# A four-layer graph network on one core: where the mean is multiplied by the reciprocal deviation, and a newly searched order of the work

## The chip, the cores and the metric

The kernel runs on one core of one Trainium2 chip. A core has five engines with queues of their own, each worked through in order: TensorE (PE in the profile; its weight loads are PEld), VectorE (DVE), ScalarE (ACT), GpSimd (POOL) and SyncE (SP), which here only issues transfers. The metric is the device time of one execution in microseconds. A measurement is the median of several executions.

## The reference

64 graphs with 256 nodes of 256 features each go through four layers. Each layer normalizes x, applies relu, and adds its result to x. Cut to what matters:

```python
def _layernorm(x, axis=-1, eps=1e-5):
    m = jnp.mean(x, axis=axis, keepdims=True)
    v = jnp.var(x, axis=axis, keepdims=True)
    return (x - m) / jnp.sqrt(v + eps)

h = jnp.maximum(_layernorm(x, axis=-1), 0.0)
x = x + _L0_gnn_ref(h, adj, ...)   # attention, 8 heads, mask from adj
h = jnp.maximum(_layernorm(x, axis=-1), 0.0)
x = x + _L1_gnn_ref(h, adj, ...)   # additive attention, softmax over axis 1, elu
h = jnp.maximum(_layernorm(x, axis=-1), 0.0)
x = x + _L2_gnn_ref(h, adj, ...)   # 3 steps of message passing and a GRU cell
h = jnp.maximum(_layernorm(x, axis=-1), 0.0)
x = x + _L3_gnn_ref(h, adj, ...)   # additive attention, 4 heads
```

So each graph is normalized four times, and a node's row needs r = 1/sqrt(v + eps) and, in one form of the scaling, also -m times r.

## The kernel before, in words

**Tiles.** Two graphs make a pair, and a pair's x is one tile of 128 partitions by 4 token groups by 256 features. The 32 pairs go through the layers 0, 1, 2 and 3. Tiles come from pools with a fixed number of buffers (6 for x, 21 for general work, `w4`, 8 PSUM banks).

**The planner.** The kernel isn't written in the order in which it runs. `Plan.add` collects tasks: an engine, a planned duration, the function that issues the instructions, and what it reads and writes. Some tasks have two forms on two engines. `Plan.ranked` decodes the string `ORDER`: three bytes for each task, two that give its place within the order and one that gives its form. `Plan.order` walks through that order once with planned durations, a time for a semaphore to reach another engine (`HOP`), a time for a transfer to land (`LANDING`, 1.2) and one port for GpSimd and those VectorE tasks that carry a `True`; from this it gives out buffers and puts filler transposes (L443) where TensorE would be idle. Then the instructions are issued in that order, each to its engine's queue. The string came from a search done outside the kernel. There are 13,776 tasks, 1788 of them TensorE's, and several pairs are under way at a time: the first TensorE task of pair 15 is number 721 of the 1788, its last is number 1013.

**Normalization** (`norm_relu`), four times for each pair, 128 times in all:

- For each of the two graphs g, VectorE computes statistics of two token groups (bn_stats, L660) and gathers them into mean and variance (bn_aggr, L662), in the tile `mv`. One task of planned 0.87 us.
- GpSimd adds eps to the variance (L673) and raises it to the power -0.5 (L674), into the first half of the tile `rs`. These are 128x4 operands, two instructions, one task of planned 1.4 us.
- VectorE multiplies the mean by -1 and by r (L679), into the second half of `rs`, a task of its own.
- x is scaled either by ScalarE as x times r plus (-m r) (L687) or by VectorE as (x - m) times r (L693).

In the last pair's layer 3 the normalization goes in two halves of two token groups each ("fine").

**After it.** In most pairs the normalized tile is transposed in blocks by VectorE (L836 and L802), written to DRAM (L791) and read back in four pieces (L794); L716 (ScalarE) or L717 (VectorE) then takes relu. L860 is the masked minimum and L867 the exponential of the attention layers. Layer 1 spreads a row to all partitions through DRAM (L1005, L1007, L1015), adds it (L1046), masks (L860), takes exponentials (L1073), divides (L1076, L1079, L1083) and multiplies on TensorE (L1096). Layer 2 holds most of the matrix work: the gates (L1219) and the messages (L1180) with their operands (L1164, L1165, L1170). L974 and L1416 are the products that read what was transposed through DRAM. Evictions of PSUM are L480 (ScalarE) and L481 (VectorE), biased ones L1235 and L1237.

**Work that may go to GpSimd.** Four additions of 512 or 256 columns are given in two forms by `either`, GpSimd or VectorE: L889 (bias in layer 0), L1282 (in the GRU), L1336 (layer 2 into x) and L1455 (layer 3 into x). The planned GpSimd time is 0.16 + 512/460 us, the planned VectorE time 0.065 + 512/960.

Of the kernel before, what the change touches and what calls it, by code (L numbers as in the profile page):

```python
# [13 lines left out]
FR = mybir.dt.float32r  # L14
# [5 lines left out]
P = 128  # L20
EPS = 1e-5
# [20 lines left out]
class Plan:  # L42
# [7 lines left out]
        "c-qBV2Y6h?)!jSudfVQ2C9SmTU2d{1x%Wl~gM)!kLJJ{;1PFly0s)fH`5_^JK!7ClUIPRhgE3$muyOCUELpv;wB^k|B4BTmy|SG|pOIFpx9`"  # L50
        "o|a_%|z4laJyhS~2__#U-mh&c*=D-ME=B}9;2Rbdvq05MpHzyzvTgzMpMfV0ut=v-$5IuF3B?O|h*5v=7ux$%poYiswfQT6gEeR;P#mugiKF"
        "5O^q^;>`eSmJ(;C%6r@$nyk?`BjS^GBvxpb-`q`^%cPUHp|BQ6e9;k^CAuIOWh#ws?BXFyjCqD0xbGu+{&rKB$y0xS@UuQ4b18U%b*!fkTAI"
        "uiMkU`Kw|InHpEy})e=I_s&Z6yy3__{3P=#<b9WjU;^+YE(xi|Y3rTc6F_!)(X!KQ+By%jpnCa^nM9elPiZN0cXLXtX94LVnD;CT`aWhzC=l"
        "~h$R>ZIE3@{q&QF{?-6eO_9JnjTd@bXy4nB`im9hztXv_+&(S49Bc8r7$4tNN$Rv)ve&Jg{u`NfD&N0Ju4Xb^$1M0S6Ib=;w8ojdB1i*g}IO"
        "NU{%TU8a^mGiwKsPh7_cJ;<ha=GfG+QtZIvD6Ho>x3x@VwPFO_4?V$oakh8Rl!J2ka7bpu13A<t#DX7XV`?`W(=?>k_8P<M=F;`~m1wL8IR+"
        "Hq&?zrqDJ0J@VWH3~GF^{82r+GS<z|QM=>^R3F(m@o9euhq>w~HIH04wMIiI=P#4hBb!dY2N%*V{>fX0XIB0=1h>-|mBM6jQtMRIpVea*SM0"
        "~jNK`&hK`#~j0m`0*Br`93F5OWxUK?z|Uq5nh{^A8XD7R{D6Ft&OvVot+WQgj~ALwb~I4N*KDD8Xx+RL|rf_O!x!?hC&8KsQbsjw#!a{8SHy"
        "p6?pB&*^qbsl+(~%8dM;`<)OPnfaDP27NUj1uffNyl~sHKg3r*o%}SFq1`-SMeiZ|cF?eDz^i#|G-Zv0fw%8T$D0QF6qg+Lu^3w}7o<}cAmR"
        "tZkV19tOOjhh|S3yKzGlrrj6E<_r0tel!8JYO%U5=gRh(l;ST~u-{+u&9dSQZeR>*oNBaz)%zmw{Qex4OGLFfO9SBC|Uo+v2l9ue4O|2Y;k3"
        "IvU`@Pb<O&9Y&tlB&N%XvQS~(j^K$e+ufZON3FR{tJ1}ys^!kY(k<n8V;(AV9Z(SKZ07>@FBu-o$dk_ngr_7YVaq)jI^Go-f~wtNmRzceBG~"  # L60
        "FJgt)ByNw?Im;M5I#RCi6JVFXZxNc2Z@Re%Cy!sKQw$wmNCQr>f5T?1?P<Si386<cCjKd`z{CI}c8b<*Zh42Dh`%qmZB4x2HD?7)XbM88D9^"
        "Iv682rsva&|Ea9axvTj6YAaTO$Gb7SI&Os95X=H)A=4Funf4Hoa8jm*4)qVLg7K~bnxb&FI^?8m+ps`XJJ2P{yyIXj2Ue1UNyFf56x=gK<E}"
        "g@Oa(hfQE(Db>^(^YXGavHVj~4JhrIrZnt&3bOp8&q!z~LddQ;Jq=;{i(r2O&;Boe&aBhPmCJIc!`7IW7G7cdQ#q?ZUf|mSE-}F1#4_<R5Y("
        "@RfkZf%YsZ#-_8}(gRmu@`mmHcQ0&%r#RGq0S)sNif<BUz9=ILRB43R?k88qD9*l2xKuCqI9OQfU2$uN3xcd_JjI2bJrAv38Df4dF`Au~)hq"
        "5OJ~m*^d$z1tSF0LaWGr(0a^J*DbdNnUk{~uHMx-dQHI&j*LbiBU@Rcm)w+(D2^@M(d2zR2t37(3SgF-m>9!M-dq$?LB@W&y9fN8W{7aIR0L"
        "b|cI3Nxx>gC=rDDJ2ecc~a9H`3<9AM0#{9ZL&)KhZGgRlegrFUGK)l^xs5#RJo-HTVwT?}>1gv;-s2!*h%01^Fu*O#6vgt2G^UxW&>s$Q7ve"
        "A3vzq|Jg%fL|L8td;)Dmm<v8>o2SbV1MDu7!@z!pcg}hbv++pSg#L%4zdCk4SXF6XV$S^_a*SU8B98a3;2_ks~yI@f`vhn(ZqSs{_HSn@>>+"
        "7@!GiCO5QGW8=s$)i^1t5O{aaWPy^_?oX<_`kPeiJ*e>w6QVm5O=yA6dZpiD*25&wEl+n~?td&Ih0Nya_d|k%Z-eu>aeyy;>5}Dg)z5UXuhz"
        "5bw&Fx@A-oM&$N4VeG!H`k7s*LWEcfeScddPI`L(zvOV>MK5%)a0O^*Z#2AO0UZrFCD89Ztb3kg-!5KtvjFX)K&I=d4cK=24S#I$eR2iPC>|"
        "U?|rv&F=usZ0+>3ws)`Gu*2p@EN6<LEWVW4R$ah~wI7VxKS$)zc9oM&s+ETK7Ma>r6Js;KHcHrP%cdUS^lIPA>lece@z?b}trY53OEo8h%1k"  # L70
# [269 lines left out]
def tile_adj_preln_d4(  # L340
# [143 lines left out]
    def either(more, do):  # L484

        return [(G, pool(N2) + more, lambda: do(nc.gpsimd), True), (V, dve(N2) + more, lambda: do(nc.vector), True)]
# [165 lines left out]
    def norm_relu(xt, p, tokens=False, turning=True):  # L652
# [3 lines left out]
        for g in range(2):  # L656

            def stats(g=g):
                for t in (2 * g, 2 * g + 1):
                    nc.vector.bn_stats(st()[:, t, :], tok(xt())[:, t, :])  # L660
                for t in (2 * g, 2 * g + 1):
                    nc.vector.bn_aggr(mv()[:, t, :], st()[:, t, :])  # L662
# [873 lines left out]
```

## Time and profile before

| what | value |
|---|---|
| median of the runs shown | 3443.62 us (4 runs, 3438.23 to 3449.06) |
| the profiled execution's own time | 3445.27 us |
| its span, first to last instruction | 3443.3 us |
| mean granted TensorE clock | 0.997 |
| TensorE busy | 3400.3 us, 99% |
| VectorE busy | 3113.5 us, 90% |
| ScalarE busy | 2450.8 us, 71% |
| GpSimd busy | 453.0 us, 13% |
| transfers | 785 MB, mean 228 GB/s |

Busy time is counted per engine; matrix instructions overlap in their pipeline, and their ends are modelled. A group line of the profile has the line of the code, the engine, the operation, the tiles and shapes and the count; behind the bar the busy time in us and the mean of one in ns; behind the second bar the time for which the engine stood idle just before these instructions, and what ended most of it. "DVE rs L679" after an arrow means: the wait ended when VectorE's instruction of line 679, which writes `rs`, was done. In a timeline, the idle time before an instruction stands in square brackets.

### The profile page before, as it was taken

The page shows a single profiled execution, that of the slowest core. Times are in us where ns is not written, and L with a number is a line of the kernel's source. Part 1 is how long each engine was busy: PE and PEld are TensorE (multiplying, and loading weights), DVE is VectorE, ACT ScalarE, POOL GpSimd, SP SyncE. Part 2 cuts the span into 40 slices and gives each one's busy share as a digit, 9 for nine tenths or more (in the row PEclk, how much of TensorE's full clock was granted, in tenths as well). Part 3 has the DMA queues.
Part 4 walks back from the last instruction along what each step waited for, and adds up shares of the span by engine and source line. Part 5 has one row for each costly group of instructions (what it writes and reads, how often), then busy time and mean ns, then how long its engine had stood idle before and what let it go on. Part 6 is the DMA issues. An engine that isn't in the chain of part 4 may idle for free. (4 is left out here: it accounts for less than half of the span.)

```text
span 3443.3 us, 55520 instructions
## 1 busy us (share of the span) xinstructions
PE 3400.3 (99%) x15701; PEld 1912.4 (56%) x15701; DVE 3113.5 (90%) x8903; ACT 2450.8 (71%) x6608; POOL 453.0 (13%) x505
## 2 busy tenths in 40 slices
PE   9999999999999999999999999999999999999998
PEld 5555555555555555555555555555555555555546
DVE  8889999998999989989999899999989999888778
ACT  8767777776677777677767776767776677766555
POOL 1100111111101111111110112111111110000100
PEclk9999999999999999999999999999999999999999
DMA  9756876887768778768778677887778776876546
GB/s 294 219 153 202 268 238 220 253 249 232 239 212 238 242 229 252 229 209 251 241 225 251 215 239 228 251 245 223 227 230 251 233 236 206 234 213 211 174 140 215
DMA packets 617687, 784.99 MB, mean 228 GB/s; under 512 B 101412, under 2 KB 524836, under 8 KB 617380
## 3 DMA queue, kind: packets, MB, share of 16 engines
q1 hardware_dynamic: 617380, 781.45, 74.0%
q8 instruction: 125, 2.05, 0.3%
q14 instruction: 182, 1.49, 0.2%
HBM read 442.51 MB, written 330.32 MB: 224 GB/s over the span
## 5 line engine op out<-in xcount | busy, mean ns | idle before, releaser
L1219 PE MATMUL ps<-w,whhT 128*128 128x512 f32 (+1 forms) x2328 | 1076.4, 591 | 2.2 <-DVE w L1293 1.1
L1219 PE MATMUL ps<-w,giT 128*128 128x512 f32 (+1 forms) x2328 | 1066.3, 588 | 0.5 <-DVE mx L860 0.3
L867 ACT ACTIVATE w<-w,mx 128x256 f32<-128x256 f32 x1536 | 758.8, 499 | 31.5 <-DVE mx L860 30.6
L1219 PEld LDWEIGHTS ps<-w,giT 128*128 128x128 f32 x2328 | 439.6, 190 | 526.1 <-issue 506.6
L1219 PEld LDWEIGHTS ps<-w,whhT 128*128 128x128 f32 x2328 | 432.7, 190 | 486.6 <-issue 439.3
L802 DVE STREAM_TRANSPOSE w<-w 128x1024 f32<-128x1024 f32 x380 | 465.9, 1230 | 31.0 <-ACT w L954 15.0
L480 ACT COPY w<-ps 128x512 f32<-128x512 f32 x476 | 267.9, 579 | 221.4 <-PE ps L1096 47.5
L860 DVE CUSTOM_DVE_ANT_0 w<-ps,mask 128x256 f32<-128x256 f32 x1024 | 373.4, 415 | 25.7 <-PE ps L922 24.3
L954 ACT ACTIVATE w<-w,rz 128x256 f32<-128x256 f32 x678 | 297.9, 500 | 83.5 <-DVE rz L948 81.0
L867 ACT ACTIVATION_READ_ACCUMULATOR w<-w,mx 128x1 f32 x1536 | 293.8, 191 | 0.0
L1282 POOL TENSOR_TENSOR w<-w,w 128x512 f32<-128x512 f32 x98 | 130.0, 1333 | 1059.1 <-ACT w L1276 835.4
L687 ACT ACTIVATE w<-x,rs 128x256 f32<-128x256 f32 x368 | 196.6, 592 | 98.3 <-DVE rs L679 95.0
L1180 PE MATMUL ps<-part,part 128*128 128x256 f32 x1536 | 252.8, 312 | 3.4 <-DVE part L1170 1.5
L1392 ACT ACTIVATE w<-w,f 128x256 f32<-128x256 f32 x512 | 224.2, 499 | 32.2 <-DMA w<-row 25.7
L1180 PEld LDWEIGHTS ps<-part,part 128*128 128x128 f32 x1536 | 201.7, 190 | 62.0 <-issue 41.3
L673 POOL TENSOR_SCALAR rs<-mv 128x4 f32<-128x4 f32 x129 | 37.2, 288 | 1481.9 <-DVE mv L662 1313.1
L1276 ACT ACTIVATE w<-w,bih_sb 128x512 f32<-128x512 f32 (+1 forms) x194 | 137.1, 712 | 113.8 <-DVE w L1272 113.2
L860 DVE CUSTOM_DVE_ANT_0 w<-w,mask 128x256 f32<-128x256 f32 x512 | 199.7, 425 | 16.9 <-ACT w L1392 15.6
L1250 ACT ACTIVATE w<-ps,brz 128x512 f32<-128x512 f32 (+1 forms) x194 | 129.9, 674 | 93.7 <-PE ps L1219 78.8
L660 DVE BATCH_NORM_STATS2 st<-x 128x6 f32<-128x256 f32 x512 | 188.8, 410 | 2.6 <-DMA x<-in_x_dram 0.5
L1264 ACT ACTIVATE w<-ps,brz 128x512 f32<-128x512 f32 (+1 forms) x194 | 130.0, 674 | 73.8 <-PE ps L1219 67.5
L1288 DVE SCALAR_TENSOR_TENSOR w<-w,w 128x512 f32<-128x512 f32 (+1 forms) x194 | 139.5, 722 | 14.8 <-ACT w L1264 9.1
(120 smaller groups left out, 5054.2 us busy)
## 6 DMA issues: line engine op xcount, KB each, us to landing
turn<-w SPq DMA_DIRECT2D x565, 512.0 KB
w<-turn SPq DMA_DIRECT2D x2260, 128.0 KB
w<-in_adj_dram SPq DMA_DIRECT2D x128, 512.0 KB
w<-row SPq DMA_DIRECT2D x64, 512.0 KB
x<-in_x_dram SPq DMA_DIRECT2D x64, 256.0 KB
out_dram<-x SPq DMA_DIRECT2D x64, 256.0 KB
turn<-w SPq DMA_DIRECT2D x62, 256.0 KB
w<-turn SPq DMA_DIRECT2D x248, 64.0 KB
```

The lines of the kernel that those rows point to most:

```text
L480: (A, act(n), lambda: nc.scalar.copy(dst(), src())),
L660: nc.vector.bn_stats(st()[:, t, :], tok(xt())[:, t, :])
L687: nc.scalar.activation(tok(xn())[:, t, :], tok(xt())[:, t, :], func, bias=rs()[:, 1, t : t + 1], scale=rs()[:, 0, t : t + 1])
L802: add((V, dve(T * N), lambda: nc.vector.transpose(blocks(), blocks())), writes=[e])
L860: nc.vector.tensor_tensor_reduce(row, src, mask, scale, 3.0e38, ALU.add, ALU.min, mn)
L867: nc.scalar.activation(row(e, r), row(e, r), AF.Exp, bias=mn()[:, r : r + 1], scale=-1.0, accum_out=zs()[:, z0(r) : z0(r) + 1])
L954: op(row(e, r), row(e, r), rz()[:, r : r + 1])
L1180: mm(ps()[:, o * N : (o + 1) * N], chunk_of(part(), h.mixed, c, o), tok(ams[g](), N)[:, c, :], start=i == 0 and c == 0, stop=i == 1 and c ...
L1219: mm(ps()[:, 0:n], w[:, k, c0 : c0 + P], of(wide(src, k)), start=i == 0, stop=i == 2 * len(terms) - 1)
L1276: (A, act(n, 1), lambda o=o: nc.scalar.activation(at(hn, o), at(hn, o), AF.Tanh, bias=bih_sb[:, 4 + o : 5 + o])),
L1288: (V, dve(n), lambda o=o, z=zt[o]: nc.vector.scalar_tensor_tensor(of(wide(u, o)), z()[:, 0:n], 1.0, of(wide(u, o)), ALU.add, ALU.mult), True),
L1392: nc.scalar.activation(dst, src, AF.Prelu, bias=f()[:, t, D + h : D + h + 1], alpha=ALPHA)
```

## The change

Four things are changed.

1. eps is added to the variance, and the mean's sign is turned, in the statistics task on VectorE: two instructions more for each graph, on 128x2 operands. The planned time goes from 0.87 to 1.0 us.
2. GpSimd's task is now the power (without the addition before it) and behind it the product of the turned mean and r, into the second half of `rs`. Its planned time goes from 1.4 to 1.7 us. The VectorE task of L679 is gone. VectorE's form of the scaling adds the turned mean where it subtracted the mean.
3. The planned time of `either`'s GpSimd form is 0.4 us longer.
4. The string `ORDER` is another one. It came from a search with GpSimd's instructions taken longer and a larger margin on every landing. `LANDING`, `HOP` and the other constants of `Plan` are as they were.

```diff
     def either(more, do):
 
-        return [(G, pool(N2) + more, lambda: do(nc.gpsimd), True), (V, dve(N2) + more, lambda: do(nc.vector), True)]
+        return [(G, pool(N2) + 0.4 + more, lambda: do(nc.gpsimd), True), (V, dve(N2) + more, lambda: do(nc.vector), True)]
...
                 for t in (2 * g, 2 * g + 1):
                     nc.vector.bn_aggr(mv()[:, t, :], st()[:, t, :])
-
-            add((V, 0.87, stats), reads=[(xt, g)], writes=[(st, g), (mv, g)])
+                nc.vector.tensor_scalar_add(mv()[:, 2 * g : 2 * g + 2, 1], mv()[:, 2 * g : 2 * g + 2, 1], EPS)
+                nc.vector.tensor_scalar_mul(mv()[:, 2 * g : 2 * g + 2, 0], mv()[:, 2 * g : 2 * g + 2, 0], -1.0)
+
+            add((V, 1.0, stats), reads=[(xt, g)], writes=[(st, g), (mv, g)])
...
             def rstd(ts=ts):
-                nc.gpsimd.tensor_scalar_add(rs()[:, 0, ts], mv()[:, ts, 1], EPS)
-                nc.gpsimd.tensor_tensor(rs()[:, 0, ts], rs()[:, 0, ts], mhalf[:, ts], ALU.pow)
+                nc.gpsimd.tensor_tensor(rs()[:, 0, ts], mv()[:, ts, 1], mhalf[:, ts], ALU.pow)
+                nc.gpsimd.tensor_tensor(rs()[:, 1, ts], mv()[:, ts, 0], rs()[:, 0, ts], ALU.mult)
 
             of = lambda b: (b, ts.start // 2) if fine else b
-            add((G, 1.4, rstd, True), reads=[of(mv)], writes=[of(rs)])
-            add(
-                (V, 0.07, lambda ts=ts: nc.vector.scalar_tensor_tensor(
-                    rs()[:, 1, ts], mv()[:, ts, 0], -1.0, rs()[:, 0, ts], ALU.mult, ALU.mult), True),
-                reads=[of(mv)], writes=[of(rs)],
-            )
+            add((G, 1.7, rstd, True), reads=[of(mv)], writes=[of(rs)])
...
                         tok(xn())[:, t, :], tok(xt())[:, t, :], mv()[:, t, 0:1], rs()[:, 0, t : t + 1],
-                        ALU.subtract, ALU.mult,
+                        ALU.add, ALU.mult,
```

The two strings, decoded with the rule in `Plan.ranked`, compare like this:

| in the order | before | changed |
|---|---|---|
| tasks | 13,776 | 13,647 |
| TensorE tasks / SP tasks | 1788 / 3611 | 1788 / 3611 |
| L889 on GpSimd / VectorE | 38 / 26 | 46 / 18 |
| L1282 on GpSimd / VectorE | 98 / 96 | 82 / 112 |
| L1336 (tasks of two instructions) on GpSimd / VectorE | 37 / 27 | 25 / 39 |
| L1455 on GpSimd / VectorE | 31 / 31 | 15 / 47 |
| biased evictions on VectorE (L1237) | 77 of 194 | 58 of 194 |
| TensorE tasks between a piece's issue (L794) and its first reader, mean | 7.23 | 7.77 |
| the same for the smaller pieces of layer 3 (L1439) | 4.30 | 5.11 |
| the same for adjacency (L772) | 7.07 | 7.28 |
| the same for spread rows (L1015) | 1.51 | 1.68 |

The first and last TensorE places of each pair differ by at most four between the two. One in twenty of the tasks has the same task behind it as before.

## The prediction

> **What bounds the kernel now.** I read the first two parts of the page, then a table of busy time over three stretches of the span, then TensorE's own waits, then the groups that the change touches, and last a timeline around the longest wait.
>
> ```profile
> span 3443.3 us, 55520 instructions
> PE 3400.3 (99%) x15701; PEld 1912.4 (56%) x15701; DVE 3113.5 (90%) x8903; ACT 2450.8 (71%) x6608; POOL 453.0 (13%) x505
> ```
>
> TensorE is busy for 3400.3 of 3443.3 us. VectorE comes next with 90%. What can be won or lost is therefore TensorE's idle time, 43.0 us, and the filler: transposes of the identity (L443) that the planner puts where it expects TensorE to stand idle.
>
> ```profile
> 0.00:200.00 200.00, 187.61 (x970) 118.02 (x971) 173.83 (x594) 148.92 (x422) 26.31 (x37) 0.98 0.81 244
> 200.00:3400.00 3200.00, 3181.94 (x14429) 1772.18 (x14428) 2904.70 (x8205) 2273.61 (x6103) 424.44 (x465) 1.00 0.74 227
> 3400.00:3443.30 43.30, 30.77 (x305) 22.25 (x304) 34.99 (x106) 28.30 (x88) 2.22 (x3) 0.94 0.74 223
> ```
>
> Each row has a stretch, its length, and then the busy time of PE, PEld, DVE, ACT and POOL. PE idles 12.4 us in the first 200 us, 18.1 us in the 3200 us between, and 12.5 us at the end. In the middle it is at 99.4%, at full clock (the column after POOL: 1.00). The filler is small:
>
> ```profile
> L443 PE MATMUL ps<-ident 128*128 128x128 f32 x85 | 10.5, 274 | 0.0
> ```
>
> So 3443.3 - 43.0 - 10.5 = 3389.8 us is matrix work. The change touches none of it: the same 1788 TensorE tasks stand in both order strings.
>
> Which wait ends last in the middle stretch? These are TensorE's waits there (us in total, times, longest):
>
> ```profile
> PE ps L1096 <- DVE dst L1373: 2.9, 1, 2.9
> PE ps L1180 <- DVE part L1170: 1.5, 3, 0.8
> PE ps L1361 <- ACT w L716: 1.5, 2, 1.0
> ...
> PE ps L1361 <- DVE w L717: 1.1, 1, 1.1
> ...
> PE ps L974 <- DMA w<-turn: 0.6, 1, 0.6
> ```
>
> They are few and short. Behind these five groups, 7.6 us, stands a transfer, directly or one step back: L716, L717 and L1165 (ahead of L1170) read what comes back through DRAM. The longest can be followed:
>
> ```profile
> 1456.58 1.70 ACT L1046 ACTIVATE w<-w,f 128x256 f32<-128x256 f32 x4 [4.05 <-DMA w<-row]
> 1463.47 0.51 ACT L1073 ACTIVATE w<-w,mx 128x256 f32<-128x256 f32 x1 [4.20 <-DVE mx L860]
> 1466.06 1.19 PE L1096 MATMUL ps<-w,w 128*128 128x256 f32 x2 [2.88 <-DVE dst L1373]
> ```
>
> ScalarE stood 4.05 us for a row from DRAM, layer 1's exponentials came late, and 9.5 us on TensorE stood 2.88 us. This is what "a larger margin on every landing" would act on.
>
> **The change part by part.** First the means times the reciprocal deviation.
>
> ```profile
> L674 POOL TENSOR_TENSOR rs<-rs,mhalf 128x4 f32<-128x4 f32 x127 | 135.2, 1065 | 10.6
> L673 POOL TENSOR_SCALAR rs<-mv 128x4 f32<-128x4 f32 x127 | 36.7, 289 | 1459.6 <-DVE mv L662 1290.8 <-DVE rz L948 85.3 <-ACT w L867 58.6
> L679 DVE SCALAR_TENSOR_TENSOR rs<-mv,rs 128x4 f32<-128x4 f32 x127 | 37.1, 292 | 39.8 <-POOL rs L674 39.6
> ```
>
> The columns after the count are busy us, mean ns of one, idle before it. *GpSimd:* it loses the addition (L673, 0.29 us) and gains a product of two 128x4 operands that the trace does not show. From below the bound is L673, 0.29 us; from above the power on the same shape, 1.065 us. I take 0.29: GpSimd's two-operand adds are 1.333 us for 512 columns (L1282) and 0.807 for 256 (L1336), a straight line that leaves 0.29 at 4 columns. So 0 (to +0.78 us) per normalization, on an engine with 13% busy.
>
> *VectorE* loses L679: 37.3 us busy in all, and 39.6 us in which its queue stood still behind L679 for GpSimd, 76.9 us together. It gains four small instructions in each of 128 normalizations, 512. The nearest rows are the three in the bias preparation:
>
> ```profile
> 115.19 0.13 DVE L594 TENSOR_TENSOR brz<-bih_sb,bhh_sb 128x4 f32<-128x4 f32 x1
> 115.36 0.17 DVE L595 TENSOR_SCALAR brz<-brz 128x4 f32<-128x4 f32 x1
> 115.44 0.16 DVE L596 TENSOR_SCALAR bhn<-bhh_sb 128x2 f32<-128x2 f32 x1
> ```
>
> From start to start an independent one takes 0.08 us (L595 to L596), one that reads the result before it 0.17 (L594 to L595). 512 of them cost 41 to 87 us; I take one of each per pair, about 0.12, so 61 us.
>
> *Forms.* The order strings say which engine takes each addition that may run on either. GpSimd's go from 204 to 168: VectorE gets 16 more of L1282 (0.685 us), 12 more of L1336 (two of 0.5 us each), 16 more of L1455 (0.745) and 8 fewer of L889 (0.673): 11.0 + 12.0 + 11.9 - 5.4 = +29.5 us. Of the evictions and scalings that ScalarE may take instead, VectorE gets 26 more copies (L481, 0.671) and 19 fewer biased ones (L1237, 0.728), which with the rest comes to about +8.
>
> *Contention.* L679 takes 157 ns in the median and up to 1246 where GpSimd works; 51 us less GpSimd work (16 x 1.333 + 24 x 0.807 + 16 x 1.34 - 8 x 1.34) can give VectorE between 0 and 51 us. I take 5, by L679's excess of (289 - 157) ns x 129 = 17 us against 172 us of GpSimd work on norms.
>
> VectorE's account: -76.9 + 61 + 29.5 + 8 - 5 = +17 us, between -49 and +48. All of it lies beside matrix work. VectorE's idle time without the waits on GpSimd is 3443.3 - 3113.5 - 39.6 = 290 us; if TensorE's 18.1 us of waits grow as that shrinks, 17/290 of them is **+1.1 us** (-3 to +3). If that cover were gone, all 17 would count.
>
> *The wait on rs.* ScalarE's scaled copies (L687) stood 95.0 us behind L679, because it sat late in VectorE's queue. Now they wait for GpSimd, right behind the power. ScalarE is 71% busy, so I count nothing; its next wait there is for VectorE's statistics. Behind a waiting L687 on ScalarE are copies out of PSUM. In the last layer, where nothing covers it, the old chain ran from GpSimd's start at 3408.19 to L693 at 3409.35. The new one adds two small VectorE instructions (0.25) and a product (0.29) and drops L673 (0.31 with its gap) and L679's 0.04: **+0.2 us** (-0.2 to +1.0).
>
> *The order.* Both strings were decoded. Pair by pair, first and last TensorE positions differ by at most four places of 1788, so the staging is the same, but only 5% of neighbours are kept. The margin can be seen: the first reader of a transposed piece (L794) stands 7.77 TensorE tasks behind its issue where it stood 7.23. At 3389.8/1788 = 1.9 us a task, that is 1.0 us more. Taking 1.0 us off each of the eight transfer-linked waits above leaves about 1.9 + 0.1 of 7.6: **-5.6 us**. For each transfer that SP issues (3611 SP tasks in both) nothing is added; the other 10.5 us of middle waits I leave as they are, though they are drawn anew.
>
> A rule of the Trainium skill speaks against the multiply's move: GPSIMD Engine Reference, section 3.1, counts 1 cycle per element on VectorE and about 2.6 on GpSimd, and keeps elementwise work on VectorE. By the rule the move only loses. In this trace L679's 289 ns on VectorE and the 289 ns that I take for GpSimd are alike at four columns, and L679's price was the 39.6 us of standing. Another speaks against the small VectorE instructions: SBUF — State Buffer, section "SBUF: two separate sides", says that a VectorE instruction in a two-port mode and a GpSimd instruction exclude each other for their whole length. By it 256 pairs, met by GpSimd in 13% of cases for half a power, would cost 256 x 0.13 x 0.53 = 18 us more of VectorE, an estimate; L679's 1246 ns agrees with its kind, and the sum would be +35 instead of +17.
>
> **The sum** is made against the profiled execution, 3445.27 us, which is 1.65 above the median of 3443.62. 3445.27 - 5.6 + 1.1 + 0.2 = 3441.0; less 1.65 that is **3439.3**, 0.13% below the median.
>
> **Rivals.** *Likeliest (0.42): no change that counts.* A measurement of this kernel can tell about 0.2%, 6.9 us; within it the time is 3436.7 to 3450.5.
>
> *Faster (0.35).* The waits that now go, VectorE's 39.6 us and ScalarE's 95.0, were also what made other feeders late, so that 8 of the remaining 12.5 us of middle waits go with them: 3445.27 - 5.6 - 8 - 1.65 = 3430. For it: nearly all of TensorE's middle waits end with VectorE or ScalarE. Against it: in the stretch from 300 to 400 us VectorE is at 96.7% and TensorE still at 99.7%, so lateness there is not what load makes. No more than the 18.1 us can go in the middle.
>
> *Slower (0.23): the additions moved to VectorE.* 44 additions (16 + 12 + 16) that GpSimd did at leisure now stand in VectorE's queue in order, 0.7 to 1.0 us each, ahead of something that TensorE reads. Place: L1282 and L1455, between gates and evictions. If one in three delays TensorE by its own 0.75 us, that is 11 us, without the landing gain 3443.6 + 11 = 3455; it decides from about one in five (6.6 us). Against it: GpSimd's adds took 1.333 us where VectorE's take 0.685, so the results come sooner.
>
> *The margin is only in the string* (inside the first case): the constant for a landing is 1.2 in both, and the readers of adjacency and of row spreads hardly moved (7.07 to 7.28 and 1.51 to 1.68 tasks). Then the 2.9 us wait may stay or return elsewhere: 3445.
>
> **How the numbers follow.** Forecast 3439.3. Range 3426 to 3458: the faster case with 4 us more, by VectorE's lower bound, and the slower one with 3 us more, by its upper one. Faster by over 0.2%: 0.35; within: 0.42; slower: 0.23.
>
> **What would show it.** GpSimd's product near 0.29 us; L679's 39.6 us of VectorE idling gone; small instructions at 0.08 to 0.17 us; GpSimd below 400 us busy; matrix work unchanged; TensorE's middle idle time near 13 us. Wrong would be a middle idle time above 25 us, TensorE waiting behind L1282 or L1455 on VectorE, or an end stretch longer than 43 us by more than 1.

## The result and the profile after

The changed kernel takes **3448.64 us** (median of 41 runs, 3445.03 to 3453.45). The kernel before, run beside it, takes 3445.22 (61 runs, 3438.23 to 3451.11). The ratio is 1.0011, with a 95% interval of 1.0006 to 1.0015: slower by about 3.4 us, where the forecast was 4.3 us faster. The profiled execution of the changed kernel took 3445.95 us, 2.7 below its median, so its trace shows only a part of the difference: its span is 0.9 us longer. The medians given below for *wide_same_plan*, *slow_gpsimd*, *new_eight_small* and *bare_new* hold one slow execution each (3555.81, 3601.02, 7649.29 and 7863.81 us), and without it they are lower by 0.4, 0.2, 0.1 and 0.5 us, which changes no reading. Line numbers moved up by one to four (L443 is now L442, L717 is L713, L794 is L790, L1219 is L1215).

The span and the engines' busy time, from the page of the changed kernel:

```profile
span 3444.2 us, 56079 instructions
PE 3407.5 (99%) x15720; PEld 1907.4 (55%) x15720; DVE 3164.6 (92%) x9350; ACT 2444.5 (71%) x6591; POOL 406.1 (12%) x457
```

TensorE's idle time fell from 43.0 to 36.7 us, and yet the span is longer: TensorE's *busy* time grew by 7.2. VectorE's grew by 51.1 us, GpSimd's fell by 46.9. By stretches, in the order of columns that the prediction explained:

```profile
0.00:200.00 200.00, 189.21 (x982) 119.63 (x983) 177.22 (x632) 145.19 (x410) 27.02 (x38) 1.00 0.79 244
200.00:3400.00 3200.00, 3185.92 (x14430) 1764.52 (x14429) 2949.86 (x8605) 2268.97 (x6089) 375.62 (x414) 1.00 0.75 227
3400.00:3444.20 44.20, 32.35 (x311) 23.26 (x310) 37.57 (x115) 30.32 (x94) 3.47 (x5) 0.95 0.68 213
```

The idle time in the middle is 3200 - 3185.9 = 14.1 us, where it was 18.1; 13 to 14 was forecast. The filler, from the groups of TensorE, is part of what TensorE gained in busy time:

```profile
L442 PE MATMUL ps<-ident 128*128 128x128 f32 x104 | 13.2, 274 | 0.0
```

That is 2.7 us more filler; the other 4.5 us are the same number of matrix instructions, taking longer in all. Like for like they take longer still. In the trace before, TensorE's granted clock was halved for 13.7 us in three places (at 45, 100 and 1465 us; the first row of the windows shows it as 0.98 before and 1.00 after), which is about 6 us of busy time lost (TensorE was busy for 12.3 of the 13.7), and the changed kernel has no such place before 3430 us. So matrix work apart from filler and clock grew by 10 to 11 us. The costliest of TensorE's waits in the middle stretch:

```profile
PE ps L1176 <- DVE part L1166: 1.4, 3, 0.9
PE ps L1215 <- DVE mx L856: 1.3, 2, 1.0
PE ps L1357 <- DVE w L713: 1.3, 1, 1.3
...
PE ps L970 <- DMA w<-turn: 0.2, 1, 0.2
```

The 2.9 us wait behind the row from DRAM is gone, and nothing above 1.3 us came in its place. The normalization's new groups (count | busy, mean ns | idle before):

```profile
L675 POOL TENSOR_TENSOR rs<-mv,rs 128x4 f32<-128x4 f32 x129 | 34.9, 271 | 10.1
L662 DVE TENSOR_SCALAR mv<-mv 128x2 f32<-128x2 f32 x256 | 47.4, 185 | 8.9
L663 DVE TENSOR_SCALAR mv<-mv 128x2 f32<-128x2 f32 x256 | 42.2, 165 | 0.0
L689 DVE TENSOR_SCALAR w<-x,mv,rs 128x256 f32<-128x256 f32 x134 | 55.4, 459 | 5.2 <-POOL rs L674 5.2
```

GpSimd's product costs 0.27 us. VectorE now stands 5.2 us for GpSimd (ahead of L689) instead of 39.6 (ahead of L679). So far nearly every line is what the prediction had asked for (GpSimd's 406.1 us missed "below 400", and the stretch behind 3400 us is 44.2 us long, a little over its sign of being wrong), and the kernel is slower. One place in the trace is worse, near the end. This is TensorE's timeline of the kernel before, and then of the changed one, in the last pair's GRU step:

```profile
3369.68 3.66 PE L1416 MATMUL ps<-w,f 128*32 128x256 f32 x64
3373.27 0.95 PE L1322 MATMUL ps<-ident,w 128*128 128x128 f32 x4
```

```profile
3369.49 1.42 PE L442 MATMUL ps<-ident 128*128 128x128 f32 x11
3371.45 0.33 PE L1318 MATMUL ps<-ident,w 128*128 128x128 f32 x1 [0.55 <-DVE w L1289]
3372.05 0.98 PE L1318 MATMUL ps<-ident,w 128*128 128x128 f32 x7 [0.27 <-DVE w L1289]
```

Before, two groups of products (L1416) cover the step. After, one of them comes behind it, and filler and two short waits stand in its place. Counting the matrix work issued up to each moment, the changed kernel is 3.0 us ahead just before 3350 us and 0.3 behind around 3380.

### The profile page after: what moved, and what is told of

Read it like the earlier page. It is cut to its first block, busy times and chain, and to the rows that moved or that the text cites. A ratio compares the mean times of both kernels' runs of the same rounds, so it can differ in the third digit from the quotient of the medians.

```text
span 3444.2 us, 56079 instructions
## 1 busy us (share of the span) xinstructions
PE 3407.5 (99%) x15720; PEld 1907.4 (55%) x15720; DVE 3164.6 (92%) x9350; ACT 2444.5 (71%) x6591; POOL 406.1 (12%) x457
## 5 line engine op out<-in xcount | busy, mean ns | idle before, releaser
L1215 PE MATMUL ps<-w,whhT 128*128 128x512 f32 (+1 forms) x2328 | 1080.4, 591 | 3.0 <-DVE mx L856 1.3
L1215 PE MATMUL ps<-w,giT 128*128 128x512 f32 (+1 forms) x2328 | 1067.7, 589 | 0.7 <-ACT w L479 0.7
L1215 PEld LDWEIGHTS ps<-w,giT 128*128 128x128 f32 x2328 | 439.7, 190 | 531.2 <-issue 510.9
L1215 PEld LDWEIGHTS ps<-w,whhT 128*128 128x128 f32 x2328 | 431.1, 190 | 471.2 <-issue 420.4
L798 DVE STREAM_TRANSPOSE w<-w 128x1024 f32<-128x1024 f32 x380 | 465.5, 1231 | 18.1 <-ACT w L863 9.8
L479 ACT COPY w<-ps 128x512 f32<-128x512 f32 x444 | 250.9, 581 | 214.9 <-PE ps L1176 61.0
L674 POOL TENSOR_TENSOR rs<-mv,mhalf 128x4 f32<-128x4 f32 x129 | 141.7, 1098 | 1719.2 <-DVE mv L663 1670.7
L1278 POOL TENSOR_TENSOR w<-w,w 128x512 f32<-128x512 f32 x82 | 107.5, 1317 | 914.2 <-ACT w L1272 560.4
```

The costliest lines, as they stand in the source:

```text
L479: (A, act(n), lambda: nc.scalar.copy(dst(), src())),
L674: nc.gpsimd.tensor_tensor(rs()[:, 0, ts], mv()[:, ts, 1], mhalf[:, ts], ALU.pow)
L798: add((V, dve(T * N), lambda: nc.vector.transpose(blocks(), blocks())), writes=[e])
L1215: mm(ps()[:, 0:n], w[:, k, c0 : c0 + P], of(wide(src, k)), start=i == 0, stop=i == 2 * len(terms) - 1)
```

## The experiments

Each was run in five rounds beside the kernel before, whose median stayed between 3444.9 and 3446.1. Three theories run through them: **E**, the end just shown costs the time; **V**, the work added on VectorE costs it, over the whole span; **F**, order, buffers and filler are fitted to each other, and the edit itself is cheap.

### The end of the order

*changed_old_end* and *old_changed_end*: each kernel with the other's order for the last 100 us of planned TensorE work.

```diff
     ORDER = (
-        ...
+        ...
     )
```

> The changed kernel with the old order for its end: the tasks behind the point from which 100 us of TensorE's planned work are left stand in the old sequence and forms. Theory E: the loss is gone, 0 us (-2 to +1) against the kernel before. Theory V: still +3 us, as nothing is changed over the first 3340 us.

> The kernel before with the new order for its end alone (the last 100 us of TensorE's planned work). Theory E: +3 to +4 us against the kernel before. Theory V: 0 us.

Measured: 3453.37 (ratio 1.0023, 1.0014 to 1.0033) and 3454.03 (1.0026, 1.0016 to 1.0035). Both are slower than both kernels. Their middles run like the kernels that they are taken from, and both lose 9 to 10 us behind the seam, where tasks stand in an order that nobody searched. A splice is no test of an end; these two are inconclusive.

*one_task_earlier* moves only the one task that the timeline shows missing.

```diff
     ORDER = (
         ...
-        transposes of L1318, ..., context task (L1412) of the last pair
+        context task (L1412) of the last pair, transposes of L1318, ...
```

> The changed kernel with one step of the end moved: the last pair's context task, with its matrix work, goes ahead of the transposes after which TensorE was seen to stand and to run filler, so that its second group of matrix work covers the last GRU step as it did before. Theory E (the end of the new order loses 3.5 to 4 us for want of this cover): about 2 to 4 us faster than the changed kernel, 3444 to 3447. Theory V (load, spread over the span): no difference to the changed kernel, 3447 to 3450, as the wait turns up behind the next group.

Measured: 3449.40 (1.0013, 1.0005 to 1.0022), the changed kernel's time. In its trace the loss before 3373 us shrank by 1 us, and behind the next group came 1.0 us of filler, which the plan, made anew, put there, and a wait of 0.5 us. Moving one task moved the loss and didn't remove it. The traces of the later runs say more about theory E; they are counted together behind the floor.

### The edit without the order

*rs_alone*: parts 1 and 2 of the change in the order of before, planned anew. *rs_same_plan*: the same instructions, but with the planned times, buffers and filler of before too (L679's task stays in the plan and issues nothing).

```diff
+                nc.vector.tensor_scalar_add(mv()[:, 2 * g : 2 * g + 2, 1], mv()[:, 2 * g : 2 * g + 2, 1], EPS)
+                nc.vector.tensor_scalar_mul(mv()[:, 2 * g : 2 * g + 2, 0], mv()[:, 2 * g : 2 * g + 2, 0], -1.0)
...
-                nc.gpsimd.tensor_scalar_add(rs()[:, 0, ts], mv()[:, ts, 1], EPS)
-                nc.gpsimd.tensor_tensor(rs()[:, 0, ts], rs()[:, 0, ts], mhalf[:, ts], ALU.pow)
+                nc.gpsimd.tensor_tensor(rs()[:, 0, ts], mv()[:, ts, 1], mhalf[:, ts], ALU.pow)
+                nc.gpsimd.tensor_tensor(rs()[:, 1, ts], mv()[:, ts, 0], rs()[:, 0, ts], ALU.mult)
...
-                (V, 0.07, lambda ts=ts: nc.vector.scalar_tensor_tensor(
-                    rs()[:, 1, ts], mv()[:, ts, 0], -1.0, rs()[:, 0, ts], ALU.mult, ALU.mult), True),
+                (V, 0.07, lambda: None, True),
...
-                        ALU.subtract, ALU.mult,
+                        ALU.add, ALU.mult,
```

(The lines on L679 are rs_same_plan's; in rs_alone its task is gone, and the planned times are the change's.)

> The edit of the normalization alone: the order before with the 129 tasks of L679 taken out of it, its forms, and the planned times of the change for the normalization. Theory E (the end of the new order costs what was lost): no difference, 0 to -2 us against the kernel before, since the end of the order is the old one. Theory V (VectorE's added small instructions and additions cost, spread over the whole span): about half of the loss, +1 to +3 us. VectorE busy about 3130 us by both.

> The whole edit of the normalization within the plan of the kernel before: the planned times are the old ones and the task of L679 is kept but issues nothing, so that every other instruction, its place, its buffers and the filler are as before. Theory F (order, buffers and filler are fitted to each other; what the edit alone lost came from a plan made with other planned times): -2 to +3 us against the kernel before. Theory V (the edit's own work on VectorE and GpSimd is the price): +12 to +16, as with the edit alone.

Measured: 3460.38 (1.0044, 1.0032 to 1.0057) and 3461.41 (1.0052, 1.0039 to 1.0064). The edit alone costs 15 to 16 us in both plans. F falls for the edit; V stands. The middle stretch of rs_same_plan and its costliest waits:

```profile
200.00:3400.00 3200.00, 3171.27 (x14350) 1759.73 (x14349) 2930.78 (x8505) 2260.22 (x6065) 429.51 (x463) 1.00 0.74 226
```

```profile
PE ps L1097 <- ACT w L1080: 3.5, 2, 2.1
PE ps L1362 <- DVE w L718: 3.3, 2, 2.3
PE ps L1097 <- DVE dst L1374: 3.1, 1, 3.1
PE ps L1181 <- DVE part L1171: 2.1, 4, 0.6
```

TensorE idles 28.7 us where it idled 18.1. No single wait is to blame: 26 waits on VectorE in this stretch, where there were 17, add up to 20.5 us where they were 12.3.

*planned_only*: the planned times of the change alone; the instructions and their order stay, buffers and filler come out differently.

```diff
-        return [(G, pool(N2) + more, lambda: do(nc.gpsimd), True), (V, dve(N2) + more, lambda: do(nc.vector), True)]
+        return [(G, pool(N2) + 0.4 + more, lambda: do(nc.gpsimd), True), (V, dve(N2) + more, lambda: do(nc.vector), True)]
...
-            add((V, 0.87, stats), reads=[(xt, g)], writes=[(st, g), (mv, g)])
+            add((V, 1.0, stats), reads=[(xt, g)], writes=[(st, g), (mv, g)])
...
-            add((G, 1.4, rstd, True), reads=[of(mv)], writes=[of(rs)])
+            add((G, 1.7, rstd, True), reads=[of(mv)], writes=[of(rs)])
```

> The kernel before with the planned times of the change alone (1.0 for 0.87, 1.7 for 1.4, 0.4 more for GpSimd's additions): the instructions and their order on each queue are the same, only the buffers that tasks are given and the filler change. Theory F: +8 to +20 us. Theory V: 0, within 2 us.

Measured: 3450.05 (1.0019, 1.0011 to 1.0028), 4.4 us. Other buffers and filler alone can move this kernel by as much as the whole change did. Its page shows 191 filler transposes (26.0 us) where the kernel before has 85 (10.5): TensorE is busy for 12.1 us more and idle for 4.3 less.

### The two halves of the edit

*four_small* adds the small VectorE instructions (as multiplications by 1.0) and leaves L679 where it is. *product_on_gpsimd* does the reverse: L679's product and the change of sign go to GpSimd, VectorE gets nothing.

```diff
+                nc.vector.tensor_scalar_mul(mv()[:, 2 * g : 2 * g + 2, 1], mv()[:, 2 * g : 2 * g + 2, 1], 1.0)
+                nc.vector.tensor_scalar_mul(mv()[:, 2 * g : 2 * g + 2, 0], mv()[:, 2 * g : 2 * g + 2, 0], 1.0)
```

```diff
                 nc.gpsimd.tensor_tensor(rs()[:, 0, ts], rs()[:, 0, ts], mhalf[:, ts], ALU.pow)
+                nc.gpsimd.tensor_tensor(rs()[:, 1, ts], mv()[:, ts, 0], rs()[:, 0, ts], ALU.mult)
+                nc.gpsimd.tensor_scalar_mul(rs()[:, 1, ts], rs()[:, 1, ts], -1.0)
...
-                (V, 0.07, lambda ts=ts: nc.vector.scalar_tensor_tensor(
-                    rs()[:, 1, ts], mv()[:, ts, 0], -1.0, rs()[:, 0, ts], ALU.mult, ALU.mult), True),
+                (V, 0.07, lambda: None, True),
```

> The kernel before with four more small VectorE instructions in each normalization (mean and variance times 1.0), L679 kept, plan unchanged: the added load alone, 512 instructions of 0.08 to 0.17 us, about 50 us of VectorE. Theory F: +1 to +5 us, what 50 us of load adds to TensorE's waits by the share of idle time that it takes. Theory V: +10 us or more.

> The kernel before with L679's product moved to GpSimd behind the power and negated there (two GpSimd instructions more), nothing added on VectorE, plan unchanged: VectorE loses 77 us of work and of standing. Theory F: -1 to -5 us if that standing was behind TensorE's waits, else 0. Theory V: -5 us or more, the mirror of the price of VectorE's load.

Measured: four_small 3474.88 (1.0090, 1.0077 to 1.0104), **29 us slower**, with VectorE's busy time up by 62.4 us; product_on_gpsimd 3439.07 (0.9986, 0.9977 to 0.9995), **6.6 us faster** than the kernel before. These are product_on_gpsimd's engines, and the group that now waits for GpSimd's power:

```profile
PE 3397.8 (99%) x15701; PEld 1910.9 (56%) x15701; DVE 3092.2 (90%) x8774; ACT 2449.4 (71%) x6608; POOL 529.9 (15%) x763
L694 DVE TENSOR_SCALAR w<-x,mv,rs 128x256 f32<-128x256 f32 x144 | 56.4, 439 | 18.4 <-POOL rs L674 18.4
```

Taking 21 us of work and 21 us of standing (39.6 to 18.4) off VectorE goes with 6.6 us; putting 62 us of work on it costs 29. A microsecond in one place of the queue is not worth what it is in another.

### The order without the edit

*order_alone*: the new order, forms and GpSimd times with the normalization of before. L679 has no place in the new string; it was put right behind GpSimd's task.

```diff
     ORDER = (
-        ...
+        ...
     )
...
-        return [(G, pool(N2) + more, lambda: do(nc.gpsimd), True), (V, dve(N2) + more, lambda: do(nc.vector), True)]
+        return [(G, pool(N2) + 0.4 + more, lambda: do(nc.gpsimd), True), (V, dve(N2) + more, lambda: do(nc.vector), True)]
```

> The new order alone, with its forms and the planned GpSimd times, on the old normalization (the tasks of L679 put right behind their GpSimd task). Theory E: +3 to +4 us against the kernel before, all of it in the last 100 us; the stretch before that level or ahead. Theory V: +1 to +3 us, spread over the span, since the additions moved to VectorE are here and the small instructions are not.

Measured: 3480.7 (1.0104, 1.0090 to 1.0118). It says little about the order: in that place VectorE stands 93.0 us for the power, in 77 waits of up to 1.5 us, where the kernel before stood 39.6. It shows what L679 can cost when it isn't put late.

*new_gpsimd*: the changed kernel, plan untouched, with all four small steps on GpSimd.

```diff
-                nc.vector.tensor_scalar_add(mv()[:, 2 * g : 2 * g + 2, 1], mv()[:, 2 * g : 2 * g + 2, 1], EPS)
-                nc.vector.tensor_scalar_mul(mv()[:, 2 * g : 2 * g + 2, 0], mv()[:, 2 * g : 2 * g + 2, 0], -1.0)
...
-                nc.gpsimd.tensor_tensor(rs()[:, 0, ts], mv()[:, ts, 1], mhalf[:, ts], ALU.pow)
+                nc.gpsimd.tensor_scalar_add(rs()[:, 0, ts], mv()[:, ts, 1], EPS)
+                nc.gpsimd.tensor_tensor(rs()[:, 0, ts], rs()[:, 0, ts], mhalf[:, ts], ALU.pow)
                 nc.gpsimd.tensor_tensor(rs()[:, 1, ts], mv()[:, ts, 0], rs()[:, 0, ts], ALU.mult)
+                nc.gpsimd.tensor_scalar_mul(rs()[:, 1, ts], rs()[:, 1, ts], -1.0)
...
-                        ALU.add, ALU.mult,
+                        ALU.subtract, ALU.mult,
```

> The changed kernel, its order, buffers and planned times untouched, with the two small VectorE instructions per group taken out: GpSimd adds eps and negates after its product (four instructions instead of two), and the VectorE form of the normalization subtracts. Theory V (VectorE's added load is the price, and the new order wins back about 12 us of the edit's 16): the load that four_small priced at 29 us is gone, so about 3439 less the 12 that the order wins, 3425 to 3430, with VectorE's busy time some 85 us lower. Theory N (the new order's worth is only that it gives the small instructions room; without them it is worth nothing): about 3439, the time of the product on GpSimd in the order of before. Theory G (GpSimd's longer chain, two instructions more, now decides): 3445 or more, with ScalarE's wait behind the negation well over 100 us.

Measured: 3438.99 (0.9983, 0.9974 to 0.9992), 9.7 us below the changed kernel, and the time of product_on_gpsimd in the order of before, to 0.1 us. Theory V's bonus for the order isn't there; the time is the one that theory N gave. VectorE's busy time is 3100.8 us, 63.8 less than the changed kernel's: the 512 small instructions take 0.125 us each.

*new_eight_small*: the same dose again, in the new order.

```diff
                 nc.vector.tensor_scalar_mul(mv()[:, 2 * g : 2 * g + 2, 0], mv()[:, 2 * g : 2 * g + 2, 0], -1.0)
+                nc.vector.tensor_scalar_mul(mv()[:, 2 * g : 2 * g + 2, 1], mv()[:, 2 * g : 2 * g + 2, 1], 1.0)
+                nc.vector.tensor_scalar_mul(mv()[:, 2 * g : 2 * g + 2, 0], mv()[:, 2 * g : 2 * g + 2, 0], 1.0)
```

> The changed kernel with the two small VectorE instructions per group followed by two more that multiply by 1.0, in the same plan: the dose of four_small a second time, in the new order. Theory V with a fixed price: as in the order of before, 29 us, about 3478. If the new order has room for such instructions (theory N, that room is what it was searched for): 10 us or less, under 3459. VectorE's busy time rises by about 62 us in either case.

Measured: 3476.07 (1.0088, 1.0073 to 1.0103). The first 512 cost 9.7 us in the new order, the second 512 cost 27.4. The order has more room for the first dose than for the second.

*old_forms*: the new order, but each task with two forms goes to the engine that it had before.

```diff
     ORDER = (
-        ...
+        ...
     )
```

> The changed kernel in its new order, but each task that may go to either of two engines goes to the one that the kernel before gave it (168 of 386 differ). The prediction charged 29.5 us of VectorE time to 36 additions that the search moved there. Theory V: VectorE's load falls by 20 to 30 us and the time by up to half of it, 3434 to 3445, if the places in the new order suit the old engines. Theory F (forms, order and buffers are fitted to each other): the time rises, 3452 or more, as in the two spliced kernels, because tasks land on an engine whose queue has no place for them there.

Measured: 3464.84 (1.0058, 1.0045 to 1.0070), 16 us slower than the changed kernel. VectorE's busy time hardly moved (3162.7), GpSimd's rose to 458.0. But the plan came out with 183 filler transposes (23.7 us) where the changed kernel has 104 (13.2), and TensorE is busy for 10.6 us more, so this run can't price the moved additions. What can is new_gpsimd: it keeps them on VectorE and takes as long as product_on_gpsimd, which doesn't. Forms and places belong together, which is what is left of theory F.

### What the small instructions cost, and why

*wide_same_plan* and *wide_new*: both small instructions once for all four columns, behind the second group's statistics, instead of twice for two: 258 instead of 512, with the same elements.

```diff
+        done, fine = [], base == "3" and p == B // 2 - 1
...
+                done.append(g)
+                sl = slice(2 * g, 2 * g + 2) if fine else slice(0, T)
+                if fine or len(done) == 2:
-                nc.vector.tensor_scalar_add(mv()[:, 2 * g : 2 * g + 2, 1], mv()[:, 2 * g : 2 * g + 2, 1], EPS)
-                nc.vector.tensor_scalar_mul(mv()[:, 2 * g : 2 * g + 2, 0], mv()[:, 2 * g : 2 * g + 2, 0], -1.0)
+                    nc.vector.tensor_scalar_add(mv()[:, sl, 1], mv()[:, sl, 1], EPS)
+                    nc.vector.tensor_scalar_mul(mv()[:, sl, 0], mv()[:, sl, 0], -1.0)
```

> The kernel rs_same_plan with its small VectorE instructions taken together: two on all four columns, behind the second group's statistics, instead of two on two columns behind each group's. The same elements in 256 instructions instead of 512. Theory L, price by the count: about 3450, as eps_only_same_plan. Price by the elements: 3461, no change. Theory C: the chain after the second group is as long as before, so no change either, 3459 to 3463.

> The changed kernel, its order and buffers untouched, with the small VectorE instructions taken together in the same way, 256 instead of 512. The 512 cost about 10 us in the new order (changed kernel against new_gpsimd). Theory L, price by the count: about 5 us less than the changed kernel, 3443 to 3445, as fast as the kernel before. Price by the elements, or theory C: no change, 3447 to 3450.

Measured: 3445.02 (0.9995, 0.9987 to 1.0004), 16.4 us below rs_same_plan; and 3440.42 (0.9985, 0.9976 to 0.9993), 8.2 us below the changed kernel and **faster than the kernel before**. wide_new's engines and its small groups:

```profile
PE 3408.1 (99%) x15720; PEld 1910.9 (56%) x15720; DVE 3133.9 (91%) x9096; ACT 2447.2 (71%) x6591; POOL 403.5 (12%) x457
L666 DVE TENSOR_SCALAR mv<-mv 128x4 f32<-128x4 f32 x129 | 23.0, 178 | 4.5
L667 DVE TENSOR_SCALAR mv<-mv 128x4 f32<-128x4 f32 x129 | 21.0, 163 | 0.0
```

Four columns take 163 to 178 ns where two took 165 to 185: the price is the instruction, not its elements. In the trace 254 instructions fewer took 30.7 us off VectorE's busy time, 0.12 us each. The Trainium skill also has a price by the instruction: Perfetto Trace Analysis, section "Optimizing Scalar/DVE Operations", gives VectorE some 60 ns of access overhead for each instruction on SBUF as engine-busy time, about twice that as profiled latency, and says that grouping can help when the engine is saturated. This case agrees with the advice; its 0.12 us of busy time is twice the page's busy figure.

*eps_only_same_plan*: rs_same_plan with the change of sign moved to GpSimd.

```diff
-                nc.vector.tensor_scalar_mul(mv()[:, 2 * g : 2 * g + 2, 0], mv()[:, 2 * g : 2 * g + 2, 0], -1.0)
...
+                nc.gpsimd.tensor_scalar_mul(rs()[:, 1, ts], rs()[:, 1, ts], -1.0)
...
-                        ALU.add, ALU.mult,
+                        ALU.subtract, ALU.mult,
```

> The kernel rs_same_plan with one of its two small VectorE instructions per group, the negation, moved to GpSimd behind the product; VectorE keeps the addition of eps: 256 small instructions instead of 512. Theory L, price by the count: half of the 22 us that rs_same_plan lies above product_on_gpsimd, about 3450. Theory C: GpSimd's chain is longer by 0.3 us where VectorE's is shorter by 0.1, so no gain, 3460 or later. A threshold (VectorE can take the first half for nothing): 3441 or less.

Measured: 3451.16 (1.0015, 1.0006 to 1.0024), as the count had it.

*slow_gpsimd*: product_on_gpsimd with a longer chain and no more VectorE work.

```diff
+                nc.gpsimd.tensor_scalar_mul(rs()[:, 1, ts], rs()[:, 1, ts], 1.0)
+                nc.gpsimd.tensor_scalar_mul(rs()[:, 1, ts], rs()[:, 1, ts], 1.0)
```

> The kernel product_on_gpsimd with two more GpSimd instructions behind the negation, each a multiplication by 1.0: the chain from the statistics to the normalization is longer by two of GpSimd's instructions, about 0.6 us each time, and VectorE has nothing more to do. In rs_same_plan the small VectorE instructions lengthened the same chain by about 0.2 us per group and cost 22 us against product_on_gpsimd. Theory C (the longer chain is the price): 22 us or more on top, 3461 or later. Theory L (VectorE's queue is the price): within 4 us of product_on_gpsimd, 3436 to 3443.

Measured: 3452.55 (1.0019, 1.0010 to 1.0028), 13.5 us more. Theory L alone is refuted: a longer chain to rs costs time although VectorE has nothing more to do (3086.7 us busy). These are ScalarE's waits behind GpSimd's rs in product_on_gpsimd, then in slow_gpsimd:

```profile
ACT w L688 <- POOL rs L676: 76.2, 42, 5.5
ACT w L690 <- POOL rs L678: 104.4, 51, 6.1
```

So the prediction's zero for that wait does not hold once the chain is lengthened. Theory C alone, at 22 us or more, doesn't fit either.

*bare_same_plan* and *bare_new*: nothing but the power and the product between statistics and scaling. Both leave out the addition of eps and the change of sign in rs's second half; they bound what these steps can cost.

```diff
-                nc.vector.tensor_scalar_add(mv()[:, 2 * g : 2 * g + 2, 1], mv()[:, 2 * g : 2 * g + 2, 1], EPS)
-                nc.vector.tensor_scalar_mul(mv()[:, 2 * g : 2 * g + 2, 0], mv()[:, 2 * g : 2 * g + 2, 0], -1.0)
...
-                        ALU.add, ALU.mult,
+                        ALU.subtract, ALU.mult,
```

> The kernel rs_same_plan without its small VectorE instructions and with nothing in their place: GpSimd's power and product are all that is left between the statistics and the scaling. It leaves work out: eps isn't added to the variance, and the second half of rs isn't negated. Theory A (prices add): two GpSimd instructions fewer than product_on_gpsimd at 6.7 us each, 3439 - 13.5 = 3425 to 3427. Theory B (a floor): 3435 to 3439, as product_on_gpsimd.

> The same in the changed kernel, its order and buffers untouched: no small VectorE instructions, GpSimd's power and product alone. It leaves work out: eps isn't added to the variance, and the second half of rs isn't negated. Theory A: wide_new has the same chain and 258 small instructions more, which at the 0.032 us between it and the changed kernel come to 8 us, so 3432. Theory B: 3436 to 3440, as wide_new and new_gpsimd.

Measured: 3436.28 (0.9972, 0.9962 to 0.9983) and 3436.35 (0.9972, 0.9961 to 0.9982). There is a floor (theory B), and it is the same in both orders. The middle stretch of bare_same_plan, then of bare_new:

```profile
200.00:3400.00 3200.00, 3184.84 (x14499) 1776.49 (x14497) 2892.99 (x8104) 2279.34 (x6118) 424.63 (x466) 1.00 0.74 228
```

```profile
200.00:3400.00 3200.00, 3190.73 (x14505) 1770.94 (x14504) 2898.72 (x8167) 2277.39 (x6113) 370.29 (x416) 1.00 0.74 228
```

The new order idles 9.3 us here where the old one idles 15.2, and gets no further by it. Over the whole span its TensorE idles 6.7 us less (3437.0 - 3405.9 = 31.1 against 3434.2 - 3396.4 = 37.8), and is busy 9.5 us longer.

**What the end costs.** The same traces, and those of the end itself, can be counted against the kernel before. Each product is taken with its usual spacing (0.43 us for 512 columns, 0.22 for 256, 0.11 for 128, 0.05 to 0.06 for the products on 32 rows or columns), filler not at all. The table says how many us earlier than the kernel before a run had issued the same amount of work, in the mean over two stretches and at the last product; spacings off by 7% move an entry by 0.1 us at most.

| trace | order | 3335 to 3350 us | 3374 to 3384 us | last product |
|---|---|---|---|---|
| changed kernel | new | 3.0 | -0.3 | -0.4 |
| new_gpsimd | new | 12.9 | 9.6 | 7.1 |
| wide_new | new | 7.8 | 4.5 | 2.6 |
| bare_new | new | 12.5 | 9.2 | 6.8 |
| product_on_gpsimd | before | 7.2 | 6.8 | 7.0 |
| bare_same_plan | before | 8.6 | 8.8 | 9.1 |
| rs_same_plan | before | -15.0 | -15.3 | -15.0 |

All four with the new order, with small instructions or without, lose 3.3 us in the last GRU step; all but the changed kernel lose 1.9 to 2.5 us more behind it. The three in the order of before lose 0.4 at most (other runs with that order up to 1.6). So theory E holds in the traces: the end of the new order costs 3.4 to 5.8 us, and takes back what the order wins before it, 3.9 us at the floor (12.5 against 8.6). Which task does so is open, as no run gave the new order a better end.

All of it in one table (medians, us; in brackets the distance from the floor of the same order; the kernel before, run beside each group, lay between 3444.9 and 3446.1, so a distance is good to about 1 us):

| between statistics and scaling | order of before | new order |
|---|---|---|
| power and product alone (bare) | 3436.28 | 3436.35 |
| two more on GpSimd | 3439.07 (+2.8) | 3438.99 (+2.6) |
| four more on GpSimd | 3452.55 (+16.3) | - |
| 258 small ones on VectorE (wide) | 3445.02 (+8.7) | 3440.42 (+4.1) |
| 256 on VectorE and one on GpSimd each time | 3451.16 (+14.9) | - |
| 512 small ones on VectorE, as in the change | 3461.41 (+25.1) | **3448.64 (+12.3)** |
| 1024 small ones on VectorE | - | 3476.07 (+39.7) |

## Why the prediction was wrong

The sum was -5.6 + 1.1 + 0.2 = -4.3 us, and the medians differ by +3.4. The time lies within the case held likeliest (3436.7 to 3450.5), but on the other side of the kernel before. In the two profiled executions the last product comes 0.4 us later: 3.0 us are won up to 3350 us, where -5.6 + 1.1 = -4.5 was forecast, and 3.4 are lost behind it, where 0.2 was. The other 2.7 us lie between the changed kernel's profiled execution and its median, and no trace shows them.

**The changes of TensorE's waits: right.** The middle idle time went from 18.1 to 14.1 us (forecast -5.6 + 1.1, so 13.6), the 2.9 us wait went, and nothing above 1.3 us came. The five groups behind a transfer fell from 7.6 to 2.9 us (forecast 2.0), the other waits went from 10.5 to 11.2. Whether the margin did this, or the new places of all tasks, no run separates. Up to 3350 us the new order is worth about what the term says: 3.9 us at the floor and 5.7 with two more steps on GpSimd (12.9 against 7.2). That matrix work would be unchanged was right for the count and wrong for the time: L1215's two groups took 5 us more in all than L1219's did, and L918 about 5 more than L922. The same shows in new_gpsimd, wide_new and bare_new, so it belongs to the order. The reason is not settled. TensorE goes from one kind of product to another 1752 times in the new order and 1692 in the old one; no run tested whether that is it.

**GpSimd's product: right,** 0.27 us for 0.29. GPSIMD Engine Reference, section 3.1, which spoke against the move, is not borne out at four columns: product_on_gpsimd moved this multiply, with one more instruction, and was 6.6 us faster.

**VectorE's account: right in its sum, partly by luck.** Forecast +17 us; measured +51.1 us busy less 34.4 us of standing (39.6 to 5.2), +16.7. The busy time had been put at +56.2 and the standing at -39.6, so two errors of 5 us cancel. The small instructions were put at 61 us and take 63.8; the prediction's estimate of 18 us more, for VectorE and GpSimd excluding each other, doesn't show in them.

**The first step that failed: "the end stretch +0.2".** That term is the chain to rs in the last layer, and that chain did not grow: from the end of bn_aggr to the scaling on VectorE it took 1.19 us where it took 1.25, since L689 doesn't wait for the product. What the sum puts at nothing is the rest of the new order's end. By the table on what the end costs, it loses 3.3 us in the last GRU step, with small instructions or without, and up to 2.5 us more behind it. This is why the order, 3.9 us ahead at the floor until 3350 us, has the same median there as the old one (3436.35 and 3436.28).

**The second step that failed: "17/290 of them is +1.1 us".** In the plan of before the edit alone costs 15 to 16 us. In the new order the account comes to -9.8 us (to the floor) + 12.3 = +2.5, near the +1.1; but that is the difference of two large amounts, neither of which is in the sum, and its nearness is luck. The step is wrong in two ways. First, it set busy time against standing time as if they were one currency. The 39.6 us of standing stood where the old plan had put L679; giving up product and standing brought 6.6 us (9.8 to the floor, with two more steps left out). The 512 small instructions stand behind every statistics task, ahead of all that VectorE does next and in the chain to rs: they cost 25 us in the old order. Second, it took the waits to grow in proportion to a mean load. The table shows a price that grows with the dose: in the new order 258 cost 4.1, 512 cost 12.3, 1024 cost 39.7, so 0.016 us for each of the first 258, 0.032 for each of the next 254 and 0.054 for each of the last 512. (The 258 are also wider and stand behind the second group alone.) The prediction had the sentence, "if that cover were gone all 17 would count", and gave it no chance: its slower rival laid the cost on the additions.

**The slower rival: the right side, the wrong place.** It laid 11 us on 44 additions moved to VectorE. No wait of TensorE behind L1278 or L1451 was seen, and new_gpsimd and bare_new, which have these additions on VectorE, take as long as their partners in the old order.

**So the change in sums:** dropping L679 and its wait, with two steps left out, takes the old kernel from 3446.1 to the floor of 3436.3, 9.8 us; the small instructions give back 25 in the old order and 12.3 in the new one, which hides half of them; what the new order wins besides, its end loses. What stays open: which part of the end loses it, how much of the small instructions' price is VectorE's queue and how much the longer chain (slow_gpsimd shows that the chain alone can cost 13.5 us), and which part of the search, the longer statistics task or the margins, gave the order its room.

## What to carry to other kernels

On an in-order queue at 90%, count the instructions that a change adds ahead of everything else, in pieces of 0.12 us, and don't pay for them with idle time removed elsewhere on the queue; measure two doses before trusting a mean share, because the price here grew with the dose. Do small per-row arithmetic once for all groups (four columns cost what two do), or on an engine with time to spare, as long as the chain stays short. Read a new order up to its last stretch as well as on the average: here it was ahead until 3350 us and lost that in the last 100. And test it again with the cheapest form of the work, since here three variants (3438.99, 3439.07 and 3440.42) beat both kernels.

## What the runs showed of the hardware

A short wait can cost TensorE more than its own length. Busy time and clock in the kernel before, around the 2.88 us wait that ends at 1466.06:

```profile
1460.00:1465.00 5.00, 3.18 (x8) 1.14 (x6) 4.89 (x13) 1.53 (x7) 0.00 (x0) 1.00 0.93 360
1465.00:1470.00 5.00, 3.94 (x9) 3.19 (x10) 1.29 (x7) 2.72 (x8) 2.48 (x2) 0.53 0.90 208
1470.00:1475.00 5.00, 5.00 (x18) 3.97 (x17) 2.75 (x5) 2.63 (x6) 0.00 (x0) 0.78 0.82 218
```

The granted clock falls to 0.5 for 6.8 us (0.53 and 0.78 in these rows), and the products behind the wait start 0.43 us apart instead of 0.22. The wait ends 0.7 us into this, so about 3 us are lost that count as *busy*; with the wait, the kernel before lost 6 us in this place. In nineteen traces (all but wide_same_plan's) there were 27 waits of 1.9 us or more between 200 and 3400 us; behind 18 of them the clock was halved for 3.4 or 6.8 us, starting 2 to 5 us after the wait began, and nowhere else in that stretch. The Trainium skill (TensorE: Matmul & The Clock Gate, section "Why this matters for your kernels") asks for no gaps above about 3 us; here gaps of 1.9 to 2.3 us were already enough in some cases. By the measurement, a wait above 2 us is the one to remove first.
